# A bound on the logits, moved from VectorE to ScalarE and GpSimd in an attention layer

## The chip, the core and the metric

The kernel runs on one core of one Trainium2 chip. The metric is the device time of one execution in microseconds (us), as the median of several runs. Engines are named as in the profile: PE (TensorE matmuls), PEld (its weight loads), DVE (VectorE), ACT (ScalarE), POOL (GpSimd), SP (SyncE, which here only issues DMAs).

## The reference

Four layers run one after the other on a batch of four images of 128 channels and 64 x 64 pixels. The change lies in layer 0 alone, an attention over the n = 4096 pixels of one image with a sparsity mask:

```python
norm = jnp.sqrt(jnp.sum(q * q, axis=0))
k = q / jnp.clip(norm, 0.0001)[None, :]
logits = jnp.einsum('cn,cm->nm', k, q)
mean = jnp.mean(logits, axis=0, keepdims=True)
sparse = jax.nn.relu(logits - mean * w[None, :] + b[None, :])
mask = (sparse != 0.0).astype(logits.dtype)
attn = jax.nn.softmax(logits * sparse * SOFTMAX_SCALE, axis=0)
attn = jnp.clip(attn * mask, 1e-08)
out = jnp.einsum('cn,nm->cm', v, attn)
```

A 3x3 convolution, a leaky ReLU and the addition of x follow. The softmax needs a number per column m that is no smaller than the largest exponent. Since k has length 1, no logit of column m is above norm(m), and no exponent above norm(m) * relu(norm(m) + ncut(m)), where ncut = b - mean * w. The kernel calls this number `bound`. Layers 1 to 3 (two state-space layers and another attention) are not touched.

## The kernel before

Layers 0 and 1 run image by image, so layer 0 has four stretches in the trace: about 57 to 700 us, 1690 to 2345, 3361 to 4018 and 5027 to 5680. In images 1 to 3 a part of layer 2 runs beside layer 0 on ACT (`beside`: two exponentials with a row sum for each tile, output `junk`).

**Chunks and tiles.** One image is cut into 8 chunks of 512 columns (`c`), and each chunk into 16 tiles of 256 rows (`m`). A tile is a pair of 128 x 512 blocks, so most instructions are 128 x 1024. The loop over `i = 16 c + m` (128 tiles and a tail) writes out, for each tile, in this order:

- `weights(i)`, DVE: `e = max(t, 0) * lg`, from the thresholded logits `t` and the logits `lg` in PSUM
- `logits(i + 2)`, PE: `lg<-q,k`, into one of two PSUM buffers
- `above(i + 1)`, DVE: `t<-lg,ncut`
- `floored(i - 18)`, DVE: `t<-t,fl`
- `shifted(i)`: for even i the Sign of the tile before on ACT (`t<-t`); POOL subtracts the bound (`e<-e,bound`); ACT takes the exponential (`e<-e`)
- `product(i - 19)`, PE: `acc<-t,vT`
- `masked(i - 1)`: `t<-t,e`, for odd tiles on POOL, for even tiles on DVE
- for even i `sums(i - 2)`, PE: `zs<-e,ones` for two tiles
- in tile 0 of a chunk the copy `z<-zs` of the last chunk's sums, on ACT
- last, steps of the side queue.

Every instruction of this loop goes through a wrapper (`InOrder`, line 111) that keeps the program's order on each engine. So line 111 stands for nearly all of them in the profile, and rows are told apart by their tiles. An engine that waits holds up all that is written behind it.

The buffers that matter: two PSUM pairs for `lg`, one PSUM bank `misc` for all side products (`th_ps`, `zt_ps`, `rz_ps`, `conv_ps`, `v_ps`), 21 buffers for `t`, four for `e`.

**The side queue.** Work that is due once a chunk is cut into steps and put into a `Queue` as runs (lists of functions). Each tile takes at most two steps that do not belong to PE and then one that does. The runs are `values(c)` (in chunk 0: `v` for the whole image), `scales` (in tiles 1 to 3: the sums' reciprocals, `fl`, `zt_ps`, `rz_ps`, `scale`), `thresholds(c + 1)` (the next chunk's `ncut` and `bound`), and from chunk 3 on `convolved(c - 3)`: six groups of taps on PE (`conv_ps`), a leaky ReLU on ACT (`y<-conv_ps,lin_b`), the addition on POOL (`y<-y,xq`) and its store by SP.

The steps of `thresholds` before the change are

```python
load, into(64, self.w1_T, "q"), hidden, into(P, kbar_rep, "q"), mean,
into(P, self.lw2_rep, "h"), times, into(P, self.bw2_rep, "h"), cut, top, top_b,
```

`into` is a PE step; `hidden` and `mean` are ACT's, `times` and `cut` DVE's. `top` is a POOL sum, `bound = own + ncut` (`own` is the norm); `top_b` is one DVE instruction, `bound = max(bound, 0) * own`. In chunks 1 to 6 `cut` and `top` fall into tile 7 and `top_b` into tile 8, together with the first group of taps where there is a convolution; its other groups follow in tiles 9 to 13, leaky ReLU, addition and store in tile 14. In chunk 0 `cut` and `top` fall into tile 5, and `top_b` into tile 6 together with the next load and product of `v`. The thresholds of chunk 0 are made before the loop. Chunk 7 makes none.

The queue already knows a step `end`, which does nothing: another queue of layer 0, `ahead`, uses it in its method `tile` to close a tile's share early. The loop over the side queue before the change doesn't look at it.

Of the kernel before, what the change touches and what calls it, by code (L numbers as in the profile page):

```python
# [10 lines left out]
AF = mybir.ActivationFunctionType  # L11
ALU = mybir.AluOpType
# [4 lines left out]
P = 128  # L17
# [12 lines left out]
class Queue:  # L30


    def __init__(self):
        self.run, self.runs, self.later = [], [], []

    def __len__(self):
        return len(self.run) + sum(len(r) for r in self.runs)
# [14 lines left out]
    def on_pe(self):  # L52

        if not self.run and self.runs:
            self.run = self.runs.pop(0)
        return bool(self.run) and getattr(self.run[0], "pe", False)
# [59 lines left out]
class Net:  # L116
# [219 lines left out]
    def layer0(self, b):  # L336
# [3 lines left out]
        pe, dve, act, pool, sp = self.pinned()  # L340
# [4 lines left out]
        with self.pool("l0", 1) as big, self.pool("l0t", 2) as tmp, self.pool("l0a", LAG + 3) as ap, \  # L345
# [6 lines left out]
            def misc(name, rows=P):  # L352
                return ps1.tile([rows, NB], F32, name=name, tag="misc")

            def row(name, bufs=2, rows=P):
                return tmp.tile([rows, NB], F32, name=name, tag=name, bufs=bufs)
# [8 lines left out]
            for c in range(0 if b else NCH):  # L365
# [11 lines left out]
                own = row("own")  # L377
# [26 lines left out]
            queue = Queue()  # L404
            held = {}
# [18 lines left out]
            qs, ncut, bound = {}, {}, {}  # L424

            def thresholds(c):


                s = bass.ts(c, NB)

                def load():
                    qs[c] = held["q"] = row("q")
                    sp.dma_start(out=qs[c], in_=self.q0[:, s])
                    held["own"] = row("own")
                    sp.dma_start(out=held["own"], in_=self.norms[:, s].to_broadcast([P, NB]))

                def into(rows, lhsT, key):
                    def go():
                        held["ps"] = misc("th_ps", rows)
                        pe.matmul(held["ps"], lhsT, held[key], start=True, stop=True)  # L440
                    return on_pe(go)

                def hidden():
                    held["h"] = row("h", 1, 64)
                    act.activation(held["h"], held["ps"], AF.Prelu, bias=self.w1_b, alpha=0.2)

                def mean():
                    held["m"] = row("m", 1)
                    act.copy(held["m"], held["ps"])

                def times():
                    dve.scalar_tensor_tensor(held["m"], held["ps"], self.lw2_b, held["m"], ALU.add, ALU.mult)

                def cut():
                    ncut[c] = row("ncut")
                    dve.scalar_tensor_tensor(ncut[c], held["ps"], self.bw2_b, held["m"], ALU.add, ALU.subtract)

                def top():
                    bound[c] = row("bound")
                    pool.tensor_tensor(bound[c], held["own"], ncut[c], ALU.add)  # L460

                def top_b():
                    dve.scalar_tensor_tensor(bound[c], bound[c], 0.0, held["own"], ALU.max, ALU.mult)

                return [
                    load, into(64, self.w1_T, "q"), hidden, into(P, kbar_rep, "q"), mean,
                    into(P, self.lw2_rep, "h"), times, into(P, self.bw2_rep, "h"), cut, top, top_b,
                ]

            def both(t):  # L470
# [4 lines left out]
            def logits(i):  # L475
                if i < S:
                    c, m = divmod(i, U)
                    lg[i] = pair()
                    for j in range(2):
                        pe.matmul(lg[i][:, j, :], k[:, bass.ts(2 * m + j, P)], qs[c], start=True, stop=True)  # L480

            def above(i):
                if i < S:
                    t[i] = ap.tile([P, 2, NB], F32, name="t", tag="t")
                    dve.tensor_tensor(t[i], lg[i], both(ncut[i // U]), ALU.add)

            def weights(i):
                e[i] = ep.tile([P, 2, NB], F32, name="e", tag="e")
                dve.scalar_tensor_tensor(e[i], t[i], 0.0, lg.pop(i), ALU.max, ALU.mult)

            def shifted(i):
                if i and i % 2 == 0:

                    act.activation(t[i - 1], t[i - 1], AF.Sign)
                pool.tensor_tensor(e[i], e[i], both(bound[i // U]), ALU.subtract)
                act.activation(e[i], e[i], AF.Exp)
# [21 lines left out]
            def floored(i):  # L518
                dve.tensor_tensor(t[i], t[i], both(floor[i // U]), ALU.max)
# [81 lines left out]

            beside = self.row_weights(b - 1, big, tmp) if b else lambda i: None
            queue.add(thresholds(0))
            if b:
                queue.step()
# [17 lines left out]
            def first_tokens():  # L623

                B = Block()
                B.b_rows, B.c_rows, B.rows = self.bc1[0, 0], self.bc1[0, 1], self.d1[0]
                x, B.u, B.delta, B.du = [flat(ap.tile([P, 2, NB], F32, name="t", tag="t")) for _ in range(4)]
                sp.dma_start(out=x, in_=self.x1[:, 0 : self.T])

                class Small:  # L630
                    def tile(self, shape, dtype, name, tag, bufs=None):
                        if name == "rs":
                            return tmp.tile(shape, dtype, name=name, tag=tag, bufs=1)
                        return row({"b": "m", "cd": "h"}[name], 1)[0 : shape[0]]

                class Parts:
                    def __init__(self):
                        self.all = [ep.tile([P, 4, NB], BF16, name="e", tag="e") for _ in range(3)]

                    def __getitem__(self, at):  # L640
                        p, i, *c = at
                        t = self.all[i][:, 0:2, :].rearrange("p a b -> p (a b)")
                        return t[p, c[0]] if c else t[p]

                def keep():
                    sp.dma_start(out=self.u1, in_=B.u)

                run = self.tokens_of(
                    B, lambda: x, lambda name, rows=P: ps2.tile([P, 2, NB], F32, name="lg", tag="lg")[0:rows, 0, :],
                    Small(), Parts, True,  # L650
                )
                B.parts = self.parts1
                return run + [keep]

            for i in range(S + LAG + 2):
                c, m = divmod(i, U)
                if i == S + 2:
                    ahead.add(first_tokens())
                if i < S:
                    weights(i)  # L660
                if i + 2 < S:
                    logits(i + 2)
                above(i + 1)
                w = i - LAG
                if 0 <= w < S:
                    floored(w)
                if i < S:
                    shifted(i)
                elif i == S:
                    act.activation(t[i - 1], t[i - 1], AF.Sign)  # L670
                beside(i)
                if i in due:
                    d = due.pop(i)
                    image(d)
                    if d:
                        queue.add(convolved(d - 1))
                    if d == NCH - 1:
                        queue.add(convolved(d))
                if 0 <= w - 1 < S:
                    product(w - 1)  # L680
                    if (w - 1) % U == U - 1:
                        due[i + 1] = (w - 1) // U
                if 0 < i <= S + 1:
                    if i <= S:
                        masked(i - 1)
                    if i % 2 == 0:
                        sums(i - 2)
                    if i % U == 0:
                        run = scales(i // U - 1)
                        run[0]()  # L690
                    elif i % U == 1 and i > U:
                        queue.first(run[1:])
                if i < S and m == 1 and c + 1 < NCH:
                    (queue.add if c else queue.first)(thresholds(c + 1))

                for _ in range(1 if i < S else 3):
                    left = 2
                    while queue and not queue.on_pe() and left:
                        queue.step()
                        left -= 1  # L700
                    if queue and queue.on_pe():
                        queue.step()
                ahead.late()
                if ahead:
                    ahead.tile(True)
# [1376 lines left out]
```

## Time and profile before

| | us |
|---|---|
| median of 3 runs | 10547.03 (10545.93 to 10552.4) |
| the profiled execution's own time | 10554.79 |
| its span, first to last instruction | 10552.9 |
| busy in the span: PE, DVE, ACT, POOL | 8461.5, 9220.4, 6330.1, 8119.2 |
| layer 0, image 0 (60 to 689): PE, DVE, ACT, POOL | 591.14, 550.21, 211.97, 466.71 of 629 |
| layer 0, image 1 (1692 to 2334): the same | 592.47, 559.78, 425.04, 465.59 of 642 |

The shares of the whole span mix layers with different limits, so the change has to be read from layer 0's own stretches. In a timeline line the columns are start and length in us, engine, line, operation, output and inputs with shapes, count, and in brackets the engine's idle time before it and what ended that. In a waits line they are the waiting engine and tile, what it waited for, the total in us, how often, and the longest. In the tile view a row gives the shortest, median and longest duration in ns and the first and last start.

### The profile page before, as it was taken

The page shows a single profiled execution, that of the slowest core. Times are in us where ns is not written, and L with a number is a line of the kernel's source. Part 1 is how long each engine was busy: PE and PEld are TensorE (multiplying, and loading weights), DVE is VectorE, ACT ScalarE, POOL GpSimd, SP SyncE. Part 2 cuts the span into 40 slices and gives each one's busy share as a digit, 9 for nine tenths or more (in the row PEclk, how much of TensorE's full clock was granted, in tenths as well). Part 3 has the DMA queues.
Part 4 walks back from the last instruction along what each step waited for, and adds up shares of the span by engine and source line. Part 5 has one row for each costly group of instructions (what it writes and reads, how often), then busy time and mean ns, then how long its engine had stood idle before and what let it go on. Part 6 is the DMA issues. An engine that isn't in the chain of part 4 may idle for free. (4 is left out here: it accounts for less than half of the span.)

```text
span 10552.9 us, 90923 instructions
## 1 busy us (share of the span) xinstructions
PE 8461.5 (80%) x27949; PEld 3020.0 (29%) x28024; DVE 9220.4 (87%) x6398; ACT 6330.1 (60%) x9496; POOL 8119.2 (77%) x3542
## 2 busy tenths in 40 slices
PE   8986667997887998887898888877777777777775
PEld 3331222332223333223333222322222222222221
DVE  7869998887998886999886999359999999999996
ACT  3334445665665665666664666456666666666765
POOL 6758886766887775887774888149999998988986
PEclk9997778998898999999999999888989989888887
DMA  1018782007875005887002888158888888888886
GB/s 37 11 42 198 189 196 82 17 13 194 207 200 148 15 13 131 199 210 192 32 15 67 200 209 199 34 134 199 204 198 208 200 204 204 216 218 220 226 224 178
DMA packets 512310, 1552.72 MB, mean 147 GB/s; under 512 B 84016, under 2 KB 91824, under 8 KB 511824
## 3 DMA queue, kind: packets, MB, share of 16 engines
q1 hardware_dynamic: 511824, 1546.92, 58.6%
q8 instruction: 222, 3.64, 0.2%
q14 instruction: 264, 2.16, 0.1%
HBM read 1349.40 MB, written 137.48 MB: 141 GB/s over the span
## 5 line engine op out<-in xcount | busy, mean ns | idle before, releaser
L111 POOL TENSOR_TENSOR p<-h,c_rep 128x1024 f32<-128x1024 f32 x2048 | 4807.9, 2357 | 831.5 <-DVE h L111 769.7
L111 DVE TENSOR_TENSOR_SCAN h<-da,carry,db 128x1024 f32<-128x1024 f32 x1536 | 3604.2, 2347 | 196.6 <-ACT da L111 17.9
L111 PE MATMUL db<-parts,sel 96*128 96x512 bf16 x4096 | 1398.2, 427 | 1499.5 <-DVE h L111 1443.9
L111 DVE TENSOR_TENSOR db<-b_rep,db 128x1024 f32<-128x1024 f32 x1536 | 1856.2, 1208 | 119.3 <-PE db L111 97.7
L111 ACT ACTIVATE da<-row,A 128x1024 f32<-128x1024 f32 x1536 | 1761.1, 1147 | 324.5 <-DMA row<-d 305.3
L111 POOL TENSOR_TENSOR e<-e,bound 128x1024 f32<-128x1024 f32 x512 | 1241.5, 2427 | 571.4 <-DVE e L111 571.1
L111 POOL TENSOR_TENSOR x<-row,b_rep 128x1024 f32<-128x1024 f32 x512 | 1208.9, 2361 | 122.8 <-DMA row<-d 122.7
L111 PE MATMUL total<-p,gather 128*32 128x512 f32 x8192 | 1246.7, 729 | 11.3 <-POOL p L111 11.2
L111 ACT ACTIVATE db<-db,A 128x1024 f32<-128x1024 f32 x512 | 555.4, 1085 | 1157.6 <-PE db L111 1093.9
L111 DVE TENSOR_TENSOR_SCAN h<-db,carry,x 128x1024 f32<-128x1024 f32 x512 | 1195.0, 2334 | 62.4 <-ACT db L111 37.9
L111 PEld LDWEIGHTS <-sel 96*128 96x128 bf16 x4096 | 308.4, 101 | 3052.8 <-DVE h L111 2062.4
L111 ACT ACTIVATE e<-e 128x1024 f32<-128x1024 f32 x512 | 540.9, 1057 | 1058.0 <-POOL e L111 1058.0
L111 PE MATMUL lg<-q,k 128*128 128x512 f32 x2048 | 1022.0, 623 | 105.8 <-DVE e L111 99.4
L111 PE MATMUL acc<-t,vT 128*128 128x512 f32 x2048 | 963.2, 594 | 3.3 <-DVE t L111 3.3
L111 PE MATMUL acc<-e,values 128*128 128x512 f32 x1536 | 855.7, 648 | 93.3 <-ACT e L111 70.3
L111 DVE TENSOR_TENSOR t<-lg,ncut 128x1024 f32<-128x1024 f32 x512 | 624.9, 1220 | 289.9 <-PE acc L111 261.3
L111 ACT ACT_TABLE_LOAD x617 | 791.6, 1283 | 39.9 <-DMA r<-y 12.3
L111 ACT COPY carry<-h 128x1 f32<-128x1 f32 x2048 | 373.8, 185 | 486.5 <-DVE h L111 482.0
L111 ACT ACTIVATE e<-gq,below,fcol 128x512 f32<-128x512 f32 x768 | 610.2, 805 | 91.0 <-PE acc L111 90.9
L111 POOL TENSOR_TENSOR t<-t,e 128x1024 f32<-128x1024 f32 x256 | 609.6, 2381 | 47.7 <-ACT t L111 47.7
L111 ACT ACTIVATE junk<-gp,ntop,fcol 128x512 f32<-128x512 f32 x768 | 619.5, 807 | 28.9 <-DMA gp<-g 16.2
L111 DVE SCALAR_TENSOR_TENSOR e<-t,lg 128x1024 f32<-128x1024 f32 x512 | 619.5, 1210 | 1.2
(257 smaller groups left out, 9887.3 us busy)
## 6 DMA issues: line engine op xcount, KB each, us to landing
row<-d SPq DMA_DIRECT2D x2048, 512.0 KB
parts<-split SPq DMA_DIRECT2D x912, 64.0 KB
b_rep<-bc SPq DMA_DIRECT2D x96, 512.0 KB
c_rep<-bc SPq DMA_DIRECT2D x96, 512.0 KB
d<-delta SPq DMA_DIRECT2D x76, 384.0 KB
r<-y SPq DMA_DIRECT2D x48, 512.0 KB
xq<-in_x SPq DMA_DIRECT2D x72, 256.0 KB
res<-x SPq DMA_DIRECT2D x32, 512.0 KB
```

The lines of the kernel that those rows point to most:

```text
L111: return self.tc.keep_in_program_order(method(*args, **kwargs))
```

## The change

The DVE step `top_b` becomes two steps: a Relu in place on ACT and a product with `own` in place on POOL. An `end` stands ahead of each of them. The loop over the side queue now closes a tile's share at an `end`: it takes no further step, and no PE step either. If a tile has used up its two steps before it meets the `end`, the mark is met first thing in the next tile and closes that one. Nothing else is changed; steps queued behind `thresholds` come correspondingly later.

```diff
     def __init__(self):
-        self.run, self.runs, self.later = [], [], []
+        self.run, self.runs, self.later, self.over = [], [], [], False
...
                 def top_b():
-                    dve.scalar_tensor_tensor(bound[c], bound[c], 0.0, held["own"], ALU.max, ALU.mult)
+                    act.activation(bound[c], bound[c], AF.Relu)
+
+                def top_c():
+                    pool.tensor_tensor(bound[c], bound[c], held["own"], ALU.mult)
 
                 return [
                     load, into(64, self.w1_T, "q"), hidden, into(P, kbar_rep, "q"), mean,
-                    into(P, self.lw2_rep, "h"), times, into(P, self.bw2_rep, "h"), cut, top, top_b,
+                    into(P, self.lw2_rep, "h"), times, into(P, self.bw2_rep, "h"), cut, top, end, top_b, end, top_c,
                 ]
...
                     while queue and not queue.on_pe() and left:
                         queue.step()
                         left -= 1
+                        if queue.over:
+                            break
+                    else:
+                        queue.over = False
+                    if queue.over:
+                        continue
                     if queue and queue.on_pe():
                         queue.step()
```

## The prediction

> **What bounds layer 0 now.** I read first the busy table by stage (windows over one chunk each), then the tile view of `bound`, then the timeline around one `bound`, then the waits. The change touches only layer 0, four stretches of about 640 us each (32 chunks of 16 tiles).
>
> Busy time by chunk; columns: length, then busy us (count) of PE, weight loads, DVE, ACT, POOL. Row 1 is a chunk without a convolution beside it, row 2 one of image 0 with it, rows 3 and 4 of image 1.
>
> ```profile
> 180.30:258.70 78.40, 72.63 (x219) 27.66 (x218) 72.70 (x63) 26.62 (x29) 57.37 (x26) 1.00 0.02 7
> 417.70:497.30 79.60, 79.51 (x237) 31.31 (x236) 69.44 (x63) 27.30 (x30) 59.24 (x28) 1.00 0.05 14
> 1972.90:2055.40 82.50, 79.80 (x237) 31.23 (x236) 71.76 (x62) 54.41 (x94) 58.72 (x27) 1.00 0.05 16
> 2055.40:2137.90 82.50, 79.82 (x237) 31.23 (x236) 71.77 (x62) 54.48 (x94) 58.73 (x27) 1.00 0.05 16
> ```
>
> Beside a convolution PE is busy for 79.8 of 82.5 us (image 0: 79.5 of 79.6): PE bounds, and DVE time is worth at most the 2.7 us that PE stands. Without one, PE and DVE are both busy for 72.6 of 78.4: something that goes round between engines bounds.
>
> ```profile
> L111 POOL TENSOR_TENSOR bound<-own,ncut x32: 1261/1276/1288, 58.3 to 5553.4; 128x512 f32<-128x512 f32 x32
> L111 DVE SCALAR_TENSOR_TENSOR bound<-bound,own x32: 684/2751/2768, 59.6 to 5557.2; 128x512 f32<-128x512 f32 x32
> ```
>
> The instruction that is moved works 0.69 us, but its median is 2.75: it waits inside itself. The timeline (start, us, engine) shows for what:
>
> ```profile
> 180.11 2.35 POOL L111 TENSOR_TENSOR t<-t,e 128x1024 f32<-128x1024 f32 x1
> 180.28 2.74 DVE L111 SCALAR_TENSOR_TENSOR bound<-bound,own 128x512 f32<-128x512 f32 x1
> 182.94 1.21 DVE L111 SCALAR_TENSOR_TENSOR e<-t,lg 128x1024 f32<-128x1024 f32 x1
> 184.32 2.36 POOL L111 TENSOR_TENSOR e<-e,bound 128x1024 f32<-128x1024 f32 x1 [1.85 <-DVE e L111]
> ...
> 191.29 2.38 POOL L111 TENSOR_TENSOR t<-t,e 128x1024 f32<-128x1024 f32 x1
> ...
> 193.62 2.36 POOL L111 TENSOR_TENSOR e<-e,bound 128x1024 f32<-128x1024 f32 x1
> ...
> 194.95 2.12 DVE L111 SCALAR_TENSOR_TENSOR t<-t,e 128x1024 f32<-128x1024 f32 x1
> ```
>
> `bound` began 0.17 us after POOL's `t<-t,e` and ended 0.56 after it. Likewise the even mask product `t<-t,e` on DVE (1.22 us alone) began at 194.95 under POOL's subtraction and ended 1.09 after it. This sets the plain period of two tiles: `e` of an even tile ready, POOL 2.36 + 2.38 + 2.36, DVE mask 1.09 after, next `e` 1.13: 9.30 us, which the ends of `e<-t,lg` in the timeline show pair after pair. The pair with `bound` takes 11.30.
>
> Last, the waits over three convolution chunks:
>
> ```profile
> DVE t L111 <- PE acc L111: 32.2, 36, 1.9
> PE lg L111 <- DVE e L111: 6.0, 6, 1.2
> PE th_ps L111 <- ACT scale L111: 2.1, 3, 0.7
> ```
>
> PE's 2.7 us a chunk are 0.84 after `bound`, 1.16 where POOL's `y<-y,xq` (it waits for the leaky ReLU) delays a subtraction, and 0.7 at `th_ps` for the `scale` copy.
>
> [...]
>
> **The change, part by part.** (1) *Removed:* 32 DVE `bound`, 4 x 0.69 before each image's loop, 4 x about 2.0 in chunk 0, 24 x about 2.75. (2) *Added:* [...]32 POOL products, priced at the sum's 1.28 (same shape and operands), 1.23 from start to start. (3) *Moved:* with the marks the Relu falls in tile 9, the product in tile 10, behind the odd mask product and ahead of tile 11's subtraction. All that follows in the queue slips two tiles: six groups of convolution taps from tiles 8-13 to 10-15, leaky ReLU, add and store from tile 14 to tile 0 of the next chunk; in chunk 0 the `v` loads and products too.
>
> (a) *Plain chunks (1 and 2 of four images, 8).* Pair 8-9 falls from 11.30 to about 9.41 (mask waiting for tile 9's subtraction). Pair 10-11 gets the product on POOL's loop: 9.30 + 1.23 = 10.53. Net -0.67, times 8 = -5.4. The Relu's own wait is over long before (the sum of tile 7); behind it on ACT stands the Sign of tile 9, which in images 1-3 still ends 0.1 before POOL's mask product needs it (exp 1.06, two row sums of 1.0, Relu 0.55 and Sign 1.04 after the subtraction's end, against POOL's 2.3 wait and next subtraction 2.36). Behind the product on POOL stands tile 11's subtraction. One race is open: tile 11's subtraction starts 0.08 + 2.32 + 2.33 + 1.23 = 5.96 after `e` of tile 10 ends, DVE's mask asks at 6.06. In the trace DVE loses when it starts 0.15 or more after POOL and wins at 0.00. At 0.10 I say it loses; if it wins, the product is hidden in POOL's idle 2.3 us: another 1.23 x 8 = -9.8.
>
> (b) *Convolution chunks of images 1-3 (3 to 6, 12).* From `e` of tile 8 ready: PE stands 1.25 before tile 12's logits (tiles 8 and 9 now have no taps to fill it), then three full pairs at 10.63, so tile 18's logits begin at 41.46 instead of 42.59: 1.1 gained. Then tile 0 of the next chunk: the leaky ReLU stands on ACT behind the copy of `z`, and that behind the `zs` sums on PE, at 46.1. Copy 0.56, ReLU 0.67, add at 47.4, tile 17's subtraction at 48.7[...]. Tile 18's subtraction starts at about 51.9, before at 51.93. The chain subtraction, exp, `scale`, `th_ps` starts there, so PE waits about 1.9 at `th_ps` instead of 0.7: what was won is given back. +0.07 each, +0.8. The store on SP now waits ahead of the next `q` and `norms` loads until about 49; they are first needed at 62, so I cost it at nothing.
>
> (c) *Convolution chunks of image 0 (4).* No layer-2 work on ACT, the add cost no PE time before. PE idles 1.25 instead of 0.84, is level at tile 18, and `th_ps` waits 0.2: +0.15 each, +0.6.
>
> (d) *Chunk 0.* There POOL's loop through exp and Sign is full. `bound` gone: -0.45 (POOL's mask product took 2.83 instead of 2.38); product +1.23; in images 1-3 the Relu lies in ACT's part of the loop, +0.6. Sum 0.8 + 3 x 1.4 = +5.0. The slipped `v` products may also move the half-clock stretches of PE that images 1-3 have near the chunk's end; unknown, from -3 to +3 an image (pair 2-3 of chunk 1 takes 12 us there against 9.5).
>
> (e) *Start of each image:* `t<-lg,ncut` no longer behind `bound`, but held by the logits: -0.1 x 4.
>
> Sum: -5.4 + 0.8 + 0.6 + 5.0 - 0.4 = +0.6. The profiled run took 10554.8 (span 10552.9 + 1.9), 7.8 above the median of 10547.0; on the median the sum gives 10547.6.
>
> **Rivals.**
> *The stall counts in full, faster.* The product hides, the shift of taps harms nothing: 24 x 1.9 less PE's floor. Plain 8 x 1.9 = 15, convolution 12 x 2.0 + 4 x 0.8 = 27, less (d) 5: about 10510. For it: 1.9 shows in every pair 8-9. Against it: PE is full beside the convolution.
> *The race is won:* 10538; within 0.2% as well.
> *The add takes the stall's place, slower.* If DVE's mask of tile 16 asks only after the add has ended, [...]tile 18 starts 1.5 later, the `scale` copy and PE with it. 16 x 1.5 = 24, with (d): 10572. It decides from about 1.3 us between ReLU's end and the mask's request; I reckon them level, which speaks against it.
> *It doesn't do what it says:* a table load before each Relu would cost ACT 1.28 (the row of table loads) twice in 32 places, at most +82. The instruction order of the changed program has none there. Under 0.01.
>
> **How the numbers follow.** A measurement can tell about 0.2% (21 us) from no change. Sum as told, race lost or won: 0.62, all within 10526-10568. Stall in full or most of it, or the clock stretches gone: 0.2. Add late, or clock stretches worse: 0.18. The range 10520 to 10568 takes in the unknown of (d) (12 us each way), the race, and the near part of both rivals.
>
> **What would show it.** Right: pair 8-9 at 9.4 and 10-11 at 10.5 in plain chunks; convolution chunks still 82.5, with PE's wait at `th_ps <- scale` grown to near 2; `y<-y,xq` in tile 0, idle before it about 3.5 behind `ACT y`; no DVE `bound`. Wrong: convolution chunks under 81.5 or above 83.5; pair 10-11 at 9.3 or less; chunk 0 unchanged.

## The result: slower by 0.6%, and the profile after

The changed kernel took 10615.19 us (median of five runs, 10605.72 to 10622.87) beside 10549.39 (10545.93 to 10559.55) for the kernel before: a ratio of 1.0060, interval 1.0046 to 1.0074. The forecast was 10547.6, with a range of 10520 to 10568. The measured time lies 47 us above that range, on the slow side, to which the prediction gave a chance of 0.18.

The profiled execution's span is 10621.1 us against 10552.9, 68.2 longer. From the first `above` to the last `e` of each loop, layer 0 took:

| us | image 0 | image 1 | image 2 | image 3 | sum |
|---|---|---|---|---|---|
| before | 627.9 | 641.7 | 643.3 | 640.8 | 2553.7 |
| after | 626.3 | 663.9 | 662.0 | 663.5 | 2615.7 |

So 62.0 of the 68.2 lie in these loops, all of it in images 1 to 3. The windows over one chunk each, with the columns as before: a plain chunk, a convolution chunk of image 0, one of image 1.

```profile
254.56:333.09 78.53, 74.25 (x219) 28.30 (x218) 71.22 (x60) 27.14 (x29) 58.57 (x27) 0.98 0.03 11
413.91:494.74 80.83, 79.57 (x237) 31.31 (x236) 71.94 (x60) 27.73 (x30) 60.80 (x28) 1.00 0.04 14
2060.08:2148.31 88.23, 82.67 (x237) 32.24 (x236) 70.79 (x60) 54.89 (x95) 61.90 (x28) 0.96 0.05 15
```

Set the last row beside the 82.5 us rows of before, which have the same 237 matmuls: the chunk is 5.7 us longer, and PE is busy for 2.9 us more, at a granted clock (PEclk, a share of full speed) of 0.96. So about half of the added time is PE standing still, and about half is PE working slowly. What has been moved is itself cheap. The tile view of `bound` (shortest/median/longest ns):

```profile
L111 POOL TENSOR_TENSOR bound<-own,ncut x32: 1264/1276/1287, 60.2 to 5626.0; 128x512 f32<-128x512 f32 x32
L111 ACT ACTIVATE bound<-bound x32: 612/613/629, 61.5 to 5637.0; 128x512 f32<-128x512 f32 x32
L111 POOL TENSOR_TENSOR bound<-bound,own x32: 1263/1288/2267, 62.2 to 5641.2; 128x512 f32<-128x512 f32 x32
```

The DVE instruction with its median of 2751 ns is gone, and in its place stand a Relu of 613 ns and a product of 1288 ns. Five rows of the waits over the 88.23 us chunk (what waited, for what, total us, times, longest):

```profile
DVE t L111 <- PE acc L111: 17.4, 10, 8.8
PE th_ps L111 <- ACT scale L111: 4.5, 1, 4.5
POOL y L111 <- ACT y L111: 3.5, 1, 3.5
POOL t L111 <- ACT t L111: 3.5, 2, 2.0
PE lg L111 <- DVE e L111: 1.0, 1, 1.0
```

PE stops once, for 4.5 us, until ACT has copied `scale`; before it was 0.7. (In chunk 7, which makes no thresholds, the product that waits for `scale` is the first `conv_ps`, for 4.5 us as well.) Three short windows of the same chunk, ahead of the stop, over it and behind it, tell what the stop does:

```profile
2111.00:2120.00 9.00, 9.00 (x36) 4.20 (x36) 7.36 (x9) 6.36 (x11) 7.47 (x4) 1.00 0.35 104
2120.00:2125.00 5.00, 0.50 (x2) 0.00 (x0) 4.02 (x4) 3.27 (x7) 3.98 (x2) 0.96 0.00 0
2125.00:2132.00 7.00, 6.99 (x9) 2.56 (x10) 0.00 (x0) 5.46 (x9) 4.65 (x2) 0.54 0.01 2
```

After it PE is busy throughout at hardly more than half its clock (PEclk 0.54), for nine matmuls in 7 us; ahead of it PEclk was 1.00.

The chain that ends at the stop is in the timeline of tiles 0 to 4 of that chunk (start and length in us, engine, line, operation, tiles, count, idle time before and its end; only the rows of the chain are shown):

```profile
2106.26 0.59 ACT L111 COPY z<-zs 128x512 f32<-128x512 f32 x1 [1.80 <-PE zs L111]
2106.74 0.69 ACT L111 ACTIVATE y<-conv_ps,lin_b 128x512 f32<-128x512 f32 x1
2107.47 1.22 DVE L111 SCALAR_TENSOR_TENSOR t<-t,e 128x1024 f32<-128x1024 f32 x1
2107.51 2.31 POOL L111 TENSOR_TENSOR y<-y,xq 128x512 f32<-128x512 f32 x1 [3.55 <-ACT y L111]
2109.79 4.68 POOL L111 TENSOR_TENSOR e<-e,bound 128x1024 f32<-128x1024 f32 x2
2112.18 1.06 ACT L111 ACTIVATE e<-e 128x1024 f32<-128x1024 f32 x1 [4.74 <-POOL e L111]
2113.14 0.80 ACT L111 ACTIVATE junk<-gp,ntop,fcol 128x512 f32<-128x512 f32 x1
2114.07 0.81 ACT L111 ACTIVATE junk<-gp,ntop,fcol 128x512 f32<-128x512 f32 x1
2114.88 1.04 ACT L111 ACTIVATE t<-t 128x1024 f32<-128x1024 f32 x1
2116.00 2.37 POOL L111 TENSOR_TENSOR t<-t,e 128x1024 f32<-128x1024 f32 x1 [1.53 <-ACT t L111]
2117.89 1.56 DVE L111 SCALAR_TENSOR_TENSOR t<-t,e 128x1024 f32<-128x1024 f32 x1
2118.33 5.65 POOL L111 TENSOR_TENSOR e<-e,bound 128x1024 f32<-128x1024 f32 x2
...
2124.40 0.56 ACT L111 COPY scale<-rz_ps 128x512 f32<-128x512 f32 x1
2125.01 1.97 PE L111 MATMUL th_ps<-q,w_T 128*64 128x512 f32 x2 [4.52 <-ACT scale L111]
```

Read downwards, each line holds up one below it. POOL stands for 3.55 us before its add, because the leaky ReLU on ACT is written behind the copy of `z`, and that waits 1.80 for PE's sums. The add begins 0.04 us behind DVE's mask and lasts 2.31 instead of 1.28. Only then come the subtractions of tiles 17 and 18 of the prediction's count (tiles 1 and 2 of the new chunk), in one row. Tile 17's exponential, two row sums of layer 2 (`junk`) and the Sign (`t<-t`) follow in line on ACT, so POOL stands again, for 1.53, before tile 17's mask product. Tile 19's subtraction follows (the first 3.34 us of the 5.65, instead of 2.35 before; a DVE mask, the row of 2117.89, overlaps its start), then its exponential and row sums on ACT, and behind them `scale`, for which PE waits.

The same points of the kernel before, in its timeline:

```profile
2107.04 2.37 POOL L111 TENSOR_TENSOR t<-t,e 128x1024 f32<-128x1024 f32 x1
2109.38 2.35 POOL L111 TENSOR_TENSOR e<-e,bound 128x1024 f32<-128x1024 f32 x1
...
2114.46 0.56 ACT L111 COPY scale<-rz_ps 128x512 f32<-128x512 f32 x1
...
2115.08 1.07 PE L111 MATMUL th_ps<-q,w_T 128*64 128x512 f32 x2 [0.68 <-ACT scale L111]
```

Set side by side, in us after `e` of tile 8 is ready (2052.78 before, 2060.08 after):

| | before | forecast | after |
|---|---|---|---|
| copy of `z` begins | 48.74 | 46.1 | 46.18 |
| add begins | in tile 14 | 47.4 | 47.43 |
| tile 17's subtraction | 47.27 | 48.7 | 49.71 |
| tile 18's subtraction | 51.93 | 51.9 | 52.0 |
| Sign of tile 17, ACT | 52.37 | not worked out | 54.80 |
| mask product of tile 17, POOL | 54.26 | not worked out | 55.92 |
| tile 19's subtraction | 56.60 | not worked out | 58.25 |
| `scale` | 61.68 | as before | 64.32 |

Everything down to tile 18's subtraction is within about 1 us of the forecast. The 2.64 us by which `scale` is late arise below that.

A measure for the experiments is the time between the ends of `e<-t,lg` two tiles apart, a "pair". The loss sits in one pair a chunk: pair 4-5 of chunks 4 to 7 in images 1 to 3, twelve pairs, lasts 16.13 on average instead of 10.27. That is 12 x 5.86 = 70 us; the rest of the loops gave back 8. (In the convolution period the other seven pairs, some longer and some shorter, add up to -0.9.)

### The profile page after: what moved, and what is told of

It is laid out like the page before. It is cut to its first block, busy times and chain, and to the rows that moved or that the text cites. A ratio compares the mean times of both kernels' runs of the same rounds, so it can differ in the third digit from the quotient of the medians.

```text
span 10621.1 us, 90964 instructions
## 1 busy us (share of the span) xinstructions
PE 8490.0 (80%) x27949; PEld 3030.9 (29%) x28024; DVE 9204.3 (87%) x6366; ACT 6345.6 (60%) x9528; POOL 8184.2 (77%) x3574
## 5 line engine op out<-in xcount | busy, mean ns | idle before, releaser
L111 PE MATMUL lg<-q,k 128*128 128x512 f32 x2048 | 1049.9, 638 | 89.8 <-DVE e L111 83.8
L111 ACT ACT_TABLE_LOAD x617 | 791.6, 1283 | 39.4 <-DMA r<-y 12.3
```

What stands on the lines that cost most here:

```text
L111: return self.tc.keep_in_program_order(method(*args, **kwargs))
```

## The experiments

**Theories.** *The slip:* the marks push leaky ReLU, add and store two tiles on, into tile 0 of the next chunk, and the chain above costs the time; the Relu and the product are innocent. *Rival, the new work:* Relu and product are too much for ACT and POOL. *Rival, the store:* the store, now ahead of the next chunk's loads in SP's queue, makes them late. Within the slip theory it was open which link of the chain decides and how much is due to the clock.

All measured values in one table: the ratio to the kernel before run beside it, with its 95% interval, the four loops' sum, the mean of the twelve pairs 4-5, and the mean convolution period in images 1 to 3 (from tile 8 to tile 8).

| | ratio [95%] | loops | pair 4-5 | conv. period |
|---|---|---|---|---|
| before | | 2553.7 | 10.27 | 82.41 |
| after | 1.0060 [1.0046, 1.0074] | 2615.7 | 16.13 | 87.41 |
| e1_no_slip | 0.9983 [0.9976, 0.9990] | 2535.5 | 10.28 | 81.36 |
| e2_dve9_slip2 | 1.0067 [1.0052, 1.0082] | 2624.7 | 16.56 | 88.46 |
| e3_dve9_slip1 | 0.9982 [0.9973, 0.9991] | 2529.7 | 10.43 | 81.33 |
| e4_dve9_slip0 | 0.9976 [0.9967, 0.9985] | 2528.7 | 10.28 | 81.35 |
| e5_no_rowsums (less work) | 0.9945 [0.9925, 0.9965] | 2493.0 | 9.30 | 80.73 |
| e6_leaky_ahead_of_z | 0.9992 [0.9985, 0.9999] | 2538.7 | 10.47 | 81.42 |
| e7_add_in_tile1 | 0.9981 [0.9973, 0.9990] | 2528.9 | 9.49 | 80.51 |
| e8_zero_products | 1.0039 [1.0025, 1.0054] | 2582.0 | 13.77 | 85.05 |
| e9_dve9_add15 | 0.9964 [0.9951, 0.9976] | 2517.3 | 10.27 | 80.24 |
| e10_before_add15 | 0.9988 [0.9982, 0.9995] | 2539.2 | 10.26 | 81.31 |

### The new work without the slip: e1_no_slip

Relu and product stand in tiles 9 and 10 (7 and 8 in chunk 0), called by the loop itself, ahead of the side queue's share (`top_b` is the Relu, `top_c` the product); in the queue one empty step keeps the place of the old `top_b`, so that nothing behind it moves.

```diff
-return [
+steps = [
...
-    into(P, self.lw2_rep, "h"), times, into(P, self.bw2_rep, "h"), cut, top, top_b,
+    into(P, self.lw2_rep, "h"), times, into(P, self.bw2_rep, "h"), cut, top,
 ]
+if c == 0:
+    return steps + [top_b, top_c]
+at = (c - 1) * U + (9 if c > 1 else 7)
+fixed[at], fixed[at + 1] = [top_b], [top_c]
+return steps + [lambda: None]
...
+for f in fixed.pop(i, ()):
+    f()
```

> The Relu on ACT and the product on POOL stay in tiles 9 and 10 (7 and 8 in chunk 0), but are called by the loop and not by the queue, so the taps stay in tiles 8 to 13 and leaky ReLU, add and store in tile 14. Theory A (the slip of the add into tile 0, behind the copy of z, makes POOL late, then ACT with its row sums, then PE): the long pairs 4-5 of 15 to 17 us vanish; plain chunks 0.67 us shorter than before, chunk 0 about 1 longer; 10530 to 10550 us. Theory B (the Relu and the product themselves are too much for ACT and POOL): as the changed kernel, 10605 to 10620.

Measured: 10536.93 us, 0.17% faster than before (10553.26), with pair 8-9 at 9.42 and pair 10-11 at 10.54, as in the changed kernel (9.41 and 10.54). Against the kernel before, the new work is no cost; it brings a little. Against e4 below, which leaves the work on DVE in tile 9, it costs about 10 us.

### The slip without the new work: e2_dve9_slip2

The one DVE instruction of before, in tile 9 by a mark, and a second mark behind it. Everything queued behind it is two tiles late, ACT and POOL do nothing new.

```diff
 def top_b():
-    act.activation(bound[c], bound[c], AF.Relu)
-
-def top_c():
-    pool.tensor_tensor(bound[c], bound[c], held["own"], ALU.mult)
+    dve.scalar_tensor_tensor(bound[c], bound[c], 0.0, held["own"], ALU.max, ALU.mult)
...
-    into(P, self.lw2_rep, "h"), times, into(P, self.bw2_rep, "h"), cut, top, end, top_b, end, top_c,
+    into(P, self.lw2_rep, "h"), times, into(P, self.bw2_rep, "h"), cut, top, end, top_b, end,
```

> bound stays one DVE instruction, in tile 9 by a mark, and a second mark behind it sends the taps to tiles 10 to 15 and leaky ReLU, add and store to tile 0, as in the changed kernel. Theory A: pairs 4-5 of chunks 4 to 7 in images 1 to 3 take 15 to 17 us, 10595 to 10615 us. Theory B: nothing added on ACT or POOL, so 10520 to 10545.

Measured: 10624.92, slower by 0.67%: the whole loss and a little more, and above the 10595 to 10615 expected. Against e4, which has the same DVE instruction in the same tile and no slip, the slip costs 98 us. Its waits over an image 1 chunk show the same two lines as the changed kernel's:

```profile
PE th_ps L111 <- ACT scale L111: 4.5, 1, 4.5
POOL y L111 <- ACT y L111: 3.6, 1, 3.6
```

With e1 this decides between the slip and the new work.

### One mark instead of two: e3_dve9_slip1

The same edit, but for the last line (the change of `top_b` and `top_c` is left out here):

```diff
-    into(P, self.lw2_rep, "h"), times, into(P, self.bw2_rep, "h"), cut, top, end, top_b, end, top_c,
+    into(P, self.lw2_rep, "h"), times, into(P, self.bw2_rep, "h"), cut, top, end, top_b,
```

> As the last one with one mark: taps in tiles 9 to 14, leaky ReLU, add and store in tile 15, ahead of the copy of z. Theory A: no long pair, 10520 to 10545 us. Theory B: the same. Theory C (what hurts is that the store waits on SP ahead of the next loads of q and the norms): tile 15 is late as well, so slower than before, 10560 or more.

Measured: 10534.48, faster by 0.18%, with pair 4-5 at 10.43. The loss depends on the second tile of slip: with one, the leaky ReLU and the add are still in the old chunk and not behind the copy of `z`. The store theory had asked for a loss here as well.

### The moved DVE instruction alone: e4_dve9_slip0

As e1, but with `bound` left on DVE, one tile later than before.

```diff
-return [
+steps = [
...
-    into(P, self.lw2_rep, "h"), times, into(P, self.bw2_rep, "h"), cut, top, top_b,
+    into(P, self.lw2_rep, "h"), times, into(P, self.bw2_rep, "h"), cut, top,
 ]
+if c == 0:
+    return steps + [top_b]
+fixed[(c - 1) * U + (9 if c > 1 else 7)] = [top_b]
+return steps + [lambda: None]
...
+for f in fixed.pop(i, ()):
+    f()
```

> bound as one DVE instruction in tile 9, called by the loop; nothing slips. It then starts after the even mask product, when POOL stands, and should take 0.7 us instead of 2.75. All theories: pair 8-9 at 9.4 and pair 10-11 at 9.9 in plain chunks, 8 x 1.3 us gained there and under 1 us in each convolution chunk, 10520 to 10540 us. It is the scale for the two before: what the slip alone costs.

Measured: 10526.55, faster by 0.24%. The tile view of `bound`:

```profile
L111 DVE SCALAR_TENSOR_TENSOR bound<-bound,own x32: 676/679/2823, 61.2 to 5539.3; 128x512 f32<-128x512 f32 x32
```

The median has fallen from 2751 to 679 ns; only the four of chunk 0 still wait (2.82 us). Pair 8-9 is 10.02 and pair 10-11 is 9.32 where 9.4 and 9.9 were expected: another split of the same sum. The stall that the change was aimed at goes away by moving the instruction one tile; no other engine is needed.

### Which link: the row sums (e5_no_rowsums)

The changed kernel without layer 2's row sums beside layer 0. This leaves out part of the computation (the sums are set to one), and with it about half of ACT's work in images 1 to 3, so its total can be set against no other kernel; what is read is pair 4-5.

```diff
+dve.memset(sums, 1.0)
...
-act.activation(
-    junk, g[0], AF.Exp, bias=ntop[:, t : t + 1], scale=self.fcol[p][:, t : t + 1],
-    accum_out=sums[:, t, c : c + 1],
-)
```

> The changed kernel without layer 2's exponentials with row sums beside layer 0 (their results are set to one, so what layer 2 makes of them is not the reference's). Theory A with ACT's row sums as a link: images 1 to 3 behave as image 0, pair 4-5 at 9.3 and each loop about 626 us from first above to last e instead of 662. Theory D (POOL's lateness alone is enough for PE's stop): pair 4-5 stays at 15 to 17 us and the loops above 650.

Measured: pair 4-5 falls to 9.30, and images 1 to 3 behave as image 0. A window over one chunk of image 1:

```profile
2040.00:2120.80 80.80, 79.57 (x238) 31.32 (x237) 71.97 (x62) 27.75 (x31) 60.76 (x27) 1.00 0.06 17
```

PE is busy for 79.57 of 80.80, with the slip in place. The rows of the chain, as above:

```profile
2089.26 2.31 POOL L111 TENSOR_TENSOR y<-y,xq 128x512 f32<-128x512 f32 x1 [3.56 <-ACT y L111]
2091.54 4.68 POOL L111 TENSOR_TENSOR e<-e,bound 128x1024 f32<-128x1024 f32 x2
2094.89 1.05 ACT L111 ACTIVATE t<-t 128x1024 f32<-128x1024 f32 x1
2096.18 2.37 POOL L111 TENSOR_TENSOR t<-t,e 128x1024 f32<-128x1024 f32 x1
2098.51 2.35 POOL L111 TENSOR_TENSOR e<-e,bound 128x1024 f32<-128x1024 f32 x1
2101.85 0.57 ACT L111 COPY scale<-rz_ps 128x512 f32<-128x512 f32 x1
```

The add is as late as in the changed kernel and lasts as long, and tiles 17 and 18 follow as there (47.41, 49.69 and 52.00 us after `e` of tile 8). But the Sign of tile 17 starts at 53.04 instead of 54.80, so the mask product doesn't wait, tile 19's subtraction is at 56.66 (before: 56.60), and `scale` isn't late. So the slip alone is harmless; it costs by way of the row sums on ACT. Image 0 of the changed kernel, which never has them, says the same (pair 4-5: 9.30).

### Which link: the leaky ReLU behind `z` (e6_leaky_ahead_of_z)

The changed kernel with the copy of `z` written behind the side queue's share in tile 0, so that the leaky ReLU doesn't wait for PE's sums.

```diff
-run[0]()                                         # z<-zs, ahead of the side queue's share
...
+if 0 < i <= S + 1 and i % U == 0:                # behind it
+    run[0]()
```

> The changed kernel with the copy of z written behind the side queue's steps of tile 0, so that the leaky ReLU does not stand behind it. Theory A (leaky ReLU behind z makes the add, and with it tile 1's subtraction, late): the add starts about 2 us earlier, pair 4-5 falls to 10 to 11, 10530 to 10555 us. If the slip hurts for another reason (two more tiles to the store, taps in tiles 14 and 15): 10600 or more.

Measured: 10543.15, 0.08% faster than before, pair 4-5 10.47. Its timeline in tile 0:

```profile
2098.28 0.67 ACT L111 ACTIVATE y<-conv_ps,lin_b 128x512 f32<-128x512 f32 x1
2099.02 1.28 POOL L111 TENSOR_TENSOR y<-y,xq 128x512 f32<-128x512 f32 x1 [1.16 <-ACT y L111]
2100.16 0.59 ACT L111 COPY z<-zs 128x512 f32<-128x512 f32 x1 [1.22 <-PE zs L111]
2100.26 2.36 POOL L111 TENSOR_TENSOR e<-e,bound 128x1024 f32<-128x1024 f32 x1
```

POOL's idle time before the add is 1.16 instead of 3.55, the add meets no DVE mask and lasts 1.28 us, and PE's wait for `scale` falls to 0.9. Two lines exchanged take back the whole loss.

### Which link: the add ahead of tile 17's subtraction (e7_add_in_tile1)

The changed kernel with a third mark, between the leaky ReLU and the add. The add then comes behind tile 17's subtraction on POOL.

```diff
-return [taps(0), taps(1, 2), taps(3), taps(4, 5), taps(6), taps(7, 8), leaky, add]
+return [taps(0), taps(1, 2), taps(3), taps(4, 5), taps(6), taps(7, 8), leaky, end, add]
```

> The changed kernel with a third mark between leaky ReLU and add: the ReLU stays in tile 0 behind z, the add goes to tile 1, behind that tile's subtraction on POOL. Theory A (what matters is that tile 1's subtraction waits on POOL behind the add): pair 4-5 at 10 to 11, 10530 to 10555 us. If ACT's order alone (ReLU behind z) is enough: as the changed kernel, 10605 to 10620.

Measured: 10530.69, 0.19% faster; pair 4-5 9.49, conv. period 80.51. A window over one chunk of image 1:

```profile
2060.00:2140.70 80.70, 79.66 (x237) 31.31 (x236) 70.54 (x61) 54.97 (x94) 61.02 (x28) 1.00 0.05 17
```

Here the leaky ReLU still stands behind `z`, and the slip is the same and more for the add. So a late leaky ReLU costs nothing by itself: what costs is POOL's waiting for it ahead of tile 17's subtraction. With that gone PE idles 1.04 us a chunk, less than the 2.68 of before (e1, where only the stall of `bound` is gone, has a period shorter than before by 1.05).

### How much is the clock: e8_zero_products

The changed kernel with filler on PE in tile 3 of chunks 4 to 7 of images 1 to 3: four products of a tile of zeros, added into `acc` (they add nothing). PE then rests for a shorter time, while `scale` stays as late as in the changed kernel.

```diff
+zero = big.tile([P, P], F32, name="zero", tag="zero")
+nc.gpsimd.memset(zero, 0.0)
...
 product(w - 1)
+if b and m == 3 and 3 < c < NCH:
+    for j in range(4):
+        pe.matmul(acc[(w - 1) // U], zero, qs[c], start=False, stop=False)
```

> The changed kernel with four products with a matrix of zeros ([...]nothing added to acc) in tile 3 of chunks 4 to 7 of images 1 to 3, where PE stands 4.5 us at th_ps. If the half clock after that stop costs 1.9 us of each long pair, as the slower lg products behind it suggest, pair 4-5 falls from 16.4 to about 14.5 and the time by 12 x 1.9 = 23 us to about 10592. If the clock plays no part: 10605 to 10620, pair 4-5 unchanged.

Measured: 10594.3, slower by 0.39%; pair 4-5 13.77. The two windows over the wait and behind it, and PE's first two rows behind the wait:

```profile
2118.00:2123.00 5.00, 3.90 (x10) 1.48 (x10) 0.26 (x1) 4.97 (x10) 2.99 (x3) 1.00 0.00 0
2123.00:2130.00 7.00, 7.00 (x23) 2.41 (x21) 5.12 (x5) 4.64 (x8) 3.22 (x2) 1.00 0.00 0
...
2119.27 1.07 PE L111 MATMUL th_ps<-q,w_T 128*64 128x512 f32 x2 [1.10 <-ACT scale L111]
2120.27 1.98 PE L111 MATMUL lg<-q,k 128*128 128x512 f32 x4
```

PE rests for 1.10 us ahead of `th_ps` instead of 4.52, and PEclk stays at 1.00. The `th_ps` products take 1.07 us instead of 1.97, and the four logits products behind them 1.98; in the changed kernel they take

```profile
2126.91 3.78 PE L111 MATMUL lg<-q,k 128*128 128x512 f32 x4
```

So of the 5.86 us a pair, 16.13 - 13.77 = 2.36 went with the half clock, about 28 us in twelve pairs, and the other 3.50 come with the longer wait. The conv. period is 2.64 above before, as much as `scale` is late.

### Better versions: e9_dve9_add15 and e10_before_add15

e7 had shown that POOL's add is worth placing. e9 is e4 with an empty step ahead of the add, which puts it into tile 15 instead of 14; e10 makes that edit alone to the kernel before.

```diff
-return [taps(0), taps(1, 2), taps(3), taps(4, 5), taps(6), taps(7, 8), leaky, add]
+return [taps(0), taps(1, 2), taps(3), taps(4, 5), taps(6), taps(7, 8), leaky, lambda: None, add]
```

> A version meant to beat both: bound as one DVE instruction in tile 9 (called by the loop, nothing slips), and the add behind the convolution one tile later, in tile 15, behind that tile's subtraction on POOL, where POOL stands anyway. If Theory A's price of the add ahead of a subtraction holds (1.2 us of PE where the add stood in tile 14), convolution chunks of images 1 to 3 fall from 81.4 (DVE in tile 9 alone) to 80.2 to 80.5, 10505 to 10522 us. If the add is hidden there already: 10525 as without it.

> The kernel before with nothing changed but the add one tile later (tile 15 instead of 14). Theory A: convolution chunks of images 1 to 3 fall from 82.5 by about 1.1, those of image 0 stay at 80.6; 10530 to 10542 us. If the add in tile 14 cost nothing: 10549.

Measured: e9 10512.26, faster than before by 0.36%, the fastest kernel here that does the whole work; e10 10539.04, by 0.12%. In loops e9 gains 36.4 us, e4 alone 25.0 and e10 alone 14.5: the two edits nearly add up. e9's chunk in image 1:

```profile
2046.48:2126.82 80.34, 79.56 (x237) 31.32 (x236) 69.25 (x61) 54.34 (x94) 58.66 (x27) 1.00 0.05 17
```

PE is busy for 79.56 of 80.34. Beside a convolution 0.8 us a chunk is left to be had, as long as PE has these products to do.

## Why the prediction was wrong, step by step

- **(a) Plain chunks: right.** Pair 8-9 at 9.41 (said 9.41), pair 10-11 at 10.54 (10.53), the race lost as said (tile 11's subtraction 5.94 to 6.00 after `e` of tile 10, the mask at 6.06). Chunk 2 of images 1 to 3 fell by 0.63 (said 0.67); only image 0's chunk 2 did not gain (78.39 to 78.53). A half-clock stretch of PE falls into it (PEclk 0.50 from 274.55 to 277.96, 0.98 over the first row above); whether that is the reason stays open.
- **(b) Convolution chunks of images 1 to 3: the step that failed.** The forecast was +0.07 each, and it became +5.0 (period 82.41 to 87.41), 12 times. Up to tile 18's subtraction the times hold, but for tile 17's subtraction, 1.0 later than said, since the mask began 0.04 ahead of the add and the add took 2.31. The error lies in the sentence "The chain subtraction, exp, `scale`, `th_ps` starts there, so PE waits about 1.9". Nothing else was looked for between tile 18's subtraction and `scale`, but POOL's mask product of tile 17 stands there. It needs tile 17's Sign, and that was behind a late exponential and two row sums on ACT. I had looked at exactly this line (exponential, row sums, Relu, Sign, mask product) for tile 9 in step (a), and not for tile 17, where the subtraction ahead of it had become 2.4 late. It cost 1.65 at tile 19's subtraction, the second overlap with a DVE mask 0.99 more (3.34 instead of 2.35). With the 1.2 that PE had gained by then (forecast 1.1), the stop became 0.68 + 2.64 + 1.2 = 4.5, as measured.
- **The clock: missed.** I took 1.9 us of idle PE as 1.9 us of loss. After the stop of 4.5 PEclk was 0.54 over 7 us, and with it came 2.4 more per chunk (e8). I had allowed for half-clock stretches at chunk 0 alone, near whose end before shows them (in image 1 PEclk 0.50 from 1777.08 to 1787.32).
- **(c) Image 0: the right way, the size missed.** Period 80.25 to 80.75, +0.5 where +0.15 was said. No row sums run there, so the long stop stays away (e5, images 1 to 3 without them: 80.73); no run takes apart where the other 0.35 comes from.
- **(d) Chunk 0: right in sum, and that by luck.** Forecast +5.0, of it +0.8 in image 0 and +1.4 in each other. The totals of chunk 0 went from 73.97, 73.23, 74.68, 73.25 to 73.04, 77.01, 75.06, 74.35: +4.3, but -0.9, +3.8, +0.4 and +1.1 one by one, inside the unknown that was stated. In e4, with neither the Relu nor the product, the same four add up to +3.6; in e10, whose chunk 0 is that of before, single ones moved by up to 1.4. So the terms of (d) are not shown. The Relu's price, 0.6 here and 0.55 in (a), was my estimate, with no Relu in the trace of before, where the copy `z<-zs` of that size took 0.56; the Relu took 0.613.
- **(e) Start of each image.** The -0.4 in sum is too small to be told from the scatter outside the loops, below.
- **The store on SP at no cost: right.** The next chunk's `q` is issued at 2110.26, 15 us before `th_ps` reads it, and e6 and e7, which keep that order, lose nothing.
- **The rivals.** "The add takes the stall's place" named the right place, the next chunk's tile 0, and the right sign. Its mechanism (tile 18 late by 1.5) and size (24 us) were not what happened: tile 18 was on time, and the loss is 12 x 5.86. "The stall counts in full" gave 10510 if the shift harmed nothing; e4, the nearest to that case, gives 10526.55 and 25.0 us in the loops. No table load appeared: the profiles of before and after both count 617 of them (ACT_TABLE_LOAD, 1283 ns each).
- **The signs.** Idle time before the add of 3.55 behind ACT's `y`: said 3.5. A wait near 2 at `th_ps`: 4.5, and chunks above 83.5 had been named as what would show the prediction wrong.

About 6 of the 68 us between the two profiled spans lie outside these loops, where the change touches only the four `bound` made ahead of them. Stretches there differ by more than that between runs (the one behind the last loop takes 4881.9 us before, 4873.5 after, 4882.0 in e10 and 4871.5 in e9), so the 6 us can be the difference of two runs; no experiment here settles it.

## What to carry to other kernels

When a step in an in-order queue slips, follow the late instruction through every engine until it meets something that PE waits for, and not only along the chain you know: ask at each engine what was queued behind it (here Sign behind exponential and row sums, then the mask product, then `scale`). A stall inside an instruction may need no other engine: one tile further on it took 0.68 us instead of 2.75 (e4), and the cheaper edit won. Look at PEclk behind a PE stop before pricing it: here 2.4 us came on top of a stop of 4.5.

## What the runs showed of the hardware

- A stop of PE of 4.5 us was followed by several microseconds at half clock (PEclk 0.54 over 7 us), with a loss of 2.4 on top. In eight of the twelve stops the half clock lasted 6.83 us (in the one shown PEclk was 0.50 from 2124.58 to 2131.41), in four 3.41. Where filler cut the rest to 1.10 us (e8), PEclk stayed at 1.00.
- A lead of 0.04 us was enough for DVE's mask product to go ahead of an operation of POOL. DVE's mask at 2107.47 went ahead with its 1.22 us, and POOL's add of 2107.51 lasted 2.31 instead of 1.28. In the whole trace of the changed kernel the mask went first in all 16 meetings where it began 0.03 or 0.04 us ahead of POOL (each time the add), and waited (about 3.3 us instead of 1.22) in all 25 where it began 0.06 to 0.15 behind (each time a subtraction). Where the mask begins while POOL runs two operations back to back, it went between them: DVE's mask at 2117.89 took 1.56 and ended at 2119.45, 1.1 after POOL's first ended, and POOL's second is recorded with 3.34 instead of 2.36; all 41 such meetings in this trace whose second operation is a subtraction went so. Both kinds of waiting lie inside the recorded lengths (2.31, 3.3 and 3.34 us), and so are counted as busy time.
